# Start-up loads held in two groups, block 2's attention put one slot earlier, and the last rows' normalization moved

## The chip, the cores and the metric

The kernel runs on one core of one Trainium2 chip. The metric is the device time of one execution in microseconds (us), taken as the median of three runs. Profiled executions are separate runs; their times stand beside their spans below.

## The reference

The input x has 2 x 2048 rows of 512 numbers. Each row goes through two steps, each with a residual:

```python
x = x + layernorm(attention(layernorm(x)))
x = x + layernorm(ffn(layernorm(x)))

# attention, 16 heads of 32:
Q = h @ Wq.T + bq;  V = h @ Wv.T + bv
logits = Q . latent_keys / sqrt(32)      # 64 latent rows for each head
w = softmax(top 4 of the logits)         # the other 60 get 0
out = (w @ latent + V) @ Wo.T + bo

# ffn, 2048 experts' columns, weights rounded to -s, 0 or +s (s = mean |W|):
out = (silu(h @ Wu.T) * (h @ Wg.T)) @ Wd.T
```

All numbers are float32.

## The kernel before

The 4096 rows are taken in 8 blocks of 512 rows, each of four tiles (t = 0 to 3) of 128 rows. Weights stay in the core's memory for the whole run.

**Order of work.** Nothing is scheduled by the compiler: each engine runs its instructions in the order in which the program issues them, and every wait stops what is queued behind it on that engine. There are three parts.

1. Start-up. Block 0's attention, the rounding of the feed-forward weights and the first pieces of block 1's attention are written out by hand, step by step, in the string FIRST_STEPS. Its names are used below: `ast` (row statistics of the input), `hold` (a one-column memset on VectorE, and behind it the weight loads, which have to wait for it), `ars` (GpSimd, 1/std), `aap` (VectorE, normalizes a row tile), `atr` (four 128x128 TensorE transposes), `acp` (copies them out of PSUM), `q`/`qc` (query product and its copy), `bh`/`bl` (split the output bias; they need the load of bo), `l`/`lc` (logits and their copy), `su`/`sg`/`sd` (ScalarE: sum of |W| of one piece of a weight), `m`, `r`, `n` (VectorE: the top 4 and the softmax), `v`, `t`, `y`, `o` (values, transposes of the weights, their product, output product).
2. For each block b, the class Experts runs 16 slots (e = 0 to 15). In a slot TensorE does `up("u", e)`, `up("g", e)` and `down(e - 1)`, each 8 matmuls: the left side is split into a high and a low part, so each product is done twice. `tanh` and the cast `high` run on ScalarE; `silu`, `gate` and `low` on VectorE. Four places (0 to 3) in each slot take pieces of the next block's attention; the function `pieces` says which piece goes where. Block b's slots therefore carry block b + 1's attention and the first row statistics of block b + 2 (`after`).
3. The tail. After the last slot come the row statistics of the last block, its normalization (`z_apply`), the residual sum and the store (`z_out`).

**Turning rows into columns.** A product needs its row tile transposed. Blocks 0 and 1 do it on TensorE, for the input (tile `pt_a`) and again for the feed-forward input (`pt_f`); so does block 2 (class SecondAttention). Blocks 3 to 7 do it off TensorE: VectorE transposes 32x32 blocks (`blocks`), a DMA writes them to memory (`far_a`, `far_f`), and another loads them in column order (`a_load` into `hT`, `f_load` into `hw`).

**Shifts.** In `pieces`, `s` is 1 for blocks 3 to 7, and 0 for blocks 1 and 2: with s = 1 the attention's pieces stand one slot earlier.

**Normalization.** `Norm.apply` does it on VectorE; `Norm.shift` (one column on VectorE) with `apply_scalar` does it on ScalarE. PSUM banks come from three pools: `at_psum` (two banks), `acc_psum` (four) and the two of `up`.

**Loads.** All go through the one queue of SyncE (SP), in program order. Before, wq is loaded right behind the four row tiles; all other weights are behind `hold`.

**Last block.** In slot 1 of block 7, `y_out` normalizes and stores the four row tiles of block 6 (lines 1128 to 1130), ahead of `F.down(0)` and `F.low(1)`.

Of the kernel before, what the change touches and what calls it, by code (L numbers as in the profile page):

```python
# [17 lines left out]
P = 128  # L18
# [16 lines left out]
FIRST_STEPS = """  # L35
ast0 hold ast1 ars0_2 ast2 ars2_3 ast3 ars3_4 aap0 aap1 atr0 aap2 atr1 acp0 aap3 atr2 acp1 atr3 acp2 acp3 q0 bh
q1 qc0 bl nst0 l0 nst3 qc1 su0 nst1 v0 lc0 nst2 lc1 nrs su2 m1 su3 m0 l1 su1 r0 q2 lc2 su5 nap0
# [21 lines left out]
def latent_attention_ternary_glu(  # L59
# [15 lines left out]
    nc = tc.nc  # L75
# [84 lines left out]
    lv = wpool.tile([P, H // 2, HP], F32, name="lv")  # L160
    nc.sync.dma_start(out=wq, in_=wqT.rearrange("(c p) n -> p c n", p=P))

    def load_weights():
        nc.sync.dma_start(out=lk, in_=latk)
        nc.sync.dma_start(out=bqv_sb, in_=bqv)
        nc.sync.dma_start(out=wv, in_=wvT.rearrange("(c p) n -> p c n", p=P))
        nc.sync.dma_start(out=lv, in_=latv)
        nc.sync.dma_start(out=bo_sb, in_=bo.to_broadcast([P, D]))
        load_x(1)
        load_up("u", wuT, (0, 2, 3, 1, 5, 6, 7, 4))  # L170
        load_up("g", wgT, (1, 2, 4, 5))
# [13 lines left out]
    nc.vector.memset(ones, 1.0)  # L185
    for i in range(16):
        nc.tensor.matmul(at_psum(f"ones_{i}")[:, :P], lhsT=ones, rhs=ones, start=True, stop=True)
# [92 lines left out]
    def row(name):  # L280
        return work.tile([P, D], F32, tag="row", name=name, bufs=4)
# [9 lines left out]
    class Attention:  # L291
# [21 lines left out]
        def a_apply(self, t):  # L313
            self.norm_a.apply(normed[self.b][:, t, :], normed[self.b][:, t, :], t)
# [224 lines left out]
    class SecondAttention(Attention):  # L539
# [23 lines left out]

        def a_apply(self, t):
            self.rows["a", t] = row(f"h_a{self.b}_{t}")
            self.norm_a.apply(self.rows["a", t], normed[self.b][:, t, :], t)

        def a_trans(self, t):
            if self.hT is None:
                self.hT = transposed("X", self.b, f"hT_{self.b}", F32)  # L570
            src = transpose_row(self.rows.pop(("a", t)), f"a{self.b}_{t}")
            nc.scalar.copy(self.hT[:, :, t * P : (t + 1) * P], src)
# [3 lines left out]
    class FirstAttention(SecondAttention):  # L576
# [7 lines left out]
        def a_trans_pe(self, t):  # L584
            if self.hT is None:
                self.hT = transposed("X", self.b, f"hT_{self.b}", F32)
            self.pt = getattr(self, "pt", {})
            self.pt[t] = transpose_row(self.rows.pop(("a", t)), f"a{self.b}_{t}")

        def a_copy(self, t):  # L590
            dst, src = self.hT[:, :, t * P : (t + 1) * P], self.pt.pop(t)
            if self.b == 0 and t == 3:
                nc.vector.tensor_copy(dst, src)
            else:
                nc.scalar.copy(dst, src)
# [130 lines left out]
    class Experts:  # L726
# [85 lines left out]
        def z_apply(self, t, n=1, i=0):  # L812
            part = slice(i * D // n, (i + 1) * D // n)
            if t < TT - 1:
                nc.scalar.activation(
                    self.y[t][:, part], self.acc[t][:, part], AF.Identity,
                    bias=self.norm.nm[:, t : t + 1], scale=self.norm.rs[:, t : t + 1],
                )
            else:
                self.norm.apply(self.y[t][:, part], self.acc[t][:, part], t)  # L820

# [56 lines left out]

    def hold_weights():
        nc.vector.memset(lk[:, 0, 0:1], 0.0)  # L880
        load_weights()

# [81 lines left out]
    def pieces(A, after):  # L964
# [5 lines left out]

        if A.b > 1:
            if A.b == 2:
                put(0, 0, A.a_apply, 0)
                put(0, 0, A.a_apply, 1)
                put(0, 1, A.a_trans, 0)
                put(0, 1, A.a_trans, 1)
                put(0, 1, A.a_apply, 2)
                put(0, 1, A.a_apply, 3)
                put(0, 2, A.a_trans, 2)
                put(0, 2, A.a_trans, 3)  # L980

        s = 1 if A.b > 2 else 0
        if A.b == 2:
            put(1, 0, A.q, 0)
            put(2, 0, A.q, 1)
            put(4, 0, A.q, 2)
            put(6, 0, A.q, 3)
        elif A.b > 2:
# [27 lines left out]
        if after is not None and after.b == 2:  # L1016
            put(14, 2, after.a_stats, 0)
            put(14, 2, after.a_stats, 1)
            put(15, 1, after.a_stats, 2)
            put(15, 1, after.a_stats, 3)  # L1020
            put(15, 1, after.a_rstd, 0, 4)
        elif after is not None:
# [11 lines left out]
        put(11 - s, 2, A.o_bias, 0)  # L1034
        for t in range(1, TT):
            put(11 - s, 2, A.o, t)
            put(11 - s, 2, A.o_bias, t)
# [23 lines left out]
        else:  # L1061
            put(12, 1, A.o_rstd, 2, 4)
            put(12, 2, A.o_apply, 0)
            put(12, 2, A.o_apply, 1)
            put(13, 0, A.o_apply, 2)
            put(13, 0, A.o_apply, 3)
            put(13, 1, A.f_stats, 0)
            put(13, 1, A.f_stats, 1)
            put(13, 1, A.f_rstd, 0, 2)
            put(13, 2, A.f_stats, 2)  # L1070
            put(13, 2, A.f_stats, 3)
            put(13, 2, A.f_rstd, 2, 4)
            put(14, 0, A.f_apply, 0)
            put(14, 0, A.f_apply, 1)
            put(14, 1, A.f_alloc)
            put(14, 1, A.f_trans, 0)
            put(14, 1, A.f_trans, 1)
            put(14, 1, A.f_apply, 2)
            put(14, 1, A.f_apply, 3)
            put(15, 0, A.f_trans, 2)  # L1080
            put(15, 0, A.f_trans, 3)
        return at

    prev = None
    for b in range(NB):
# [5 lines left out]
        for e in range(EC):  # L1091
            if e == 4 and 0 < b < NB - 1:
                load_x(b + 1)
            if e == (12 if b == 0 else 6) and b + 2 < NB:
                load_normed(b + 2)
# [51 lines left out]
            if e > 0 or b < NB - 1:  # L1147
                F.low(e)
        prev = F

# [78 lines left out]
```

## Time and profile before

| what | value |
|---|---|
| median of 3 runs | 1149.09 us (1148.38 to 1149.38) |
| profiled execution | 1152.65 us, of which the span on the core is 1150.6 us |
| TensorE (PE) busy | 1134.1 us, 99% |
| VectorE (DVE) busy | 840.3 us, 73% |
| ScalarE (ACT) busy | 402.2 us, 35% |
| GpSimd (POOL) busy | 167.8 us, 15% |
| mean granted TensorE clock | 0.996 |

Times inside the profile are microseconds from the span's start. The chain of work that ended last is 93% TensorE. A group "x8" in the chain is 8 matmuls of one tile.

### The profile page before, as it was taken

What the parts mean: (1) busy time and instruction counts of PE and PEld (TensorE: products, weight loads), DVE (VectorE), ACT (ScalarE), POOL (GpSimd) and SP (SyncE); (2) the same over time, 40 slices, a digit from 0 to 9 for tenths busy, and PEclk for the clock granted to TensorE, in tenths of its full rate; (3) what the DMA queues carried; (4) which work ended last, traced back from release to release, by engine and by line L of the source; (5) the groups of instructions that cost most, each with busy time, mean ns of one, the idle gap of its engine ahead of it and who ended that gap; (6) DMA issues with size and microseconds to landing.
All of it is one profiled execution on the core that took longest, in us unless ns stands there. A gap on an engine that the chain in (4) does not pass through costs nothing.

```text
span 1150.6 us, 14497 instructions
## 1 busy us (share of the span) xinstructions
PE 1134.1 (99%) x4650; PEld 776.1 (67%) x4650; DVE 840.3 (73%) x2940; ACT 402.2 (35%) x701; POOL 167.8 (15%) x205
## 2 busy tenths in 40 slices
PE   8999999999999999999999999999999999999997
PEld 5547675776757676676657766586675776768785
DVE  5977984967966878668876788677886787847435
ACT  3995541333213322333214333143322333224223
POOL 1057001310022100320003200022002120031100
PEclk8999999999999999999999999999999999999999
DMA  9700211022211322132222232232321412102001
GB/s 350 299 0 11 65 65 46 1 95 98 65 37 37 120 83 86 43 110 92 92 74 74 74 101 92 65 97 69 115 69 55 111 67 92 62 1 74 37 1 37
DMA packets 89355, 90.87 MB, mean 79 GB/s; under 512 B 7872, under 2 KB 62400, under 8 KB 89280
## 3 DMA queue, kind: packets, MB, share of 16 engines
q1 hardware_dynamic: 89280, 89.95, 24.5%
q8 instruction: 37, 0.61, 0.2%
q14 instruction: 38, 0.31, 0.1%
HBM read 56.37 MB, written 33.55 MB: 78 GB/s over the span
## 4 chain that ended last, share of the span: by engine, by line
PE 93%; DVE 4%; DMA 1%; ACT 1%; issue 0%; SPq 0%; POOL 0%; DVEq 0%; ACTq 0%
PE pg L740 19%; PE pu L740 19%; PE acc L783 19%; PE po L468 8%; PE pv L440 8%; PE pq L353 7%; PE pv L457 3%; PE pl L367 2%; PE pq L601 2%; PE po L692 1%; PE pv L646 1%; DMA hT<-far_a 1%; DVE left L393 1%; DMA x<-in_x 0%; PE pt_f L286 0%; DVE lo L773 0%
## 5 line engine op out<-in xcount | busy, mean ns | idle before, releaser
L740 PE MATMUL pg<-hT_f,tern_g 128*128 128x512 f32 x512 | 208.1, 406 | 0.0
L740 PE MATMUL pu<-hT_f,tern_u 128*128 128x512 f32 x512 | 204.4, 400 | 0.0
L783 PE MATMUL acc<-tern_d,hi 128*128 128x512 f32 x512 | 203.6, 398 | 0.0
L783 PE MATMUL acc<-tern_d,lo 128*128 128x512 f32 x512 | 200.0, 391 | 2.2 <-DVE lo L773 2.1
L740 PE MATMUL pg<-lT_f,tern_g 128*128 128x512 f32 x512 | 199.6, 390 | 0.0
L740 PE MATMUL pu<-lT_f,tern_u 128*128 128x512 f32 x512 | 198.9, 389 | 0.0
L749 ACT ACTIVATE h<-pu,columns 128x512 f32<-128x512 f32 x128 | 87.1, 681 | 200.3 <-PE pu L740 200.1
L768 ACT CAST hi<-h 128x512 fp32r<-128x512 f32 x128 | 79.2, 619 | 216.8 <-DVE h L757 216.8
L752 DVE SCALAR_TENSOR_TENSOR h<-h,pu 128x512 f32<-128x512 f32 x128 | 85.9, 671 | 86.7 <-ACT h L749 86.7
L757 DVE TENSOR_TENSOR h<-h,pg 128x512 f32<-128x512 f32 x128 | 86.4, 675 | 66.2 <-PE pg L740 65.2
L783 PEld LDWEIGHTS acc<-tern_d,hi 128*128 128x128 f32 x512 | 96.1, 188 | 32.7 <-issue 13.4
L740 PEld LDWEIGHTS pg<-hT_f,tern_g 128*128 128x128 f32 x512 | 96.1, 188 | 25.3 <-issue 1.9
L783 PEld LDWEIGHTS acc<-tern_d,lo 128*128 128x128 f32 x512 | 96.2, 188 | 24.5 <-DVE lo L773 4.1
L740 PEld LDWEIGHTS pu<-hT_f,tern_u 128*128 128x128 f32 x512 | 96.1, 188 | 24.6 <-issue 2.6
L740 PEld LDWEIGHTS pu<-lT_f,tern_u 128*128 128x128 f32 x512 | 96.1, 188 | 22.4 <-issue 2.9
L740 PEld LDWEIGHTS pg<-lT_f,tern_g 128*128 128x128 f32 x512 | 96.2, 188 | 22.1 <-issue 3.3
L773 DVE TENSOR_TENSOR lo<-h,hi 128x512 fp32r<-128x512 f32 x128 | 92.3, 721 | 25.5 <-ACT hi L768 25.5
L440 PE MATMUL pv<-hT,wv 128*128 128x512 f32 x224 | 100.7, 592 | 0.1
L393 DVE MATCH_REPLACE8 left<-m,w 128x64 f32<-128x64 f32 x512 | 100.3, 210 | 0.0
L468 PE MATMUL po<-wo,attnT 128*128 128x512 f32 x224 | 97.3, 592 | 0.0
L353 PE MATMUL pq<-hT,wq 128*128 128x512 f32 x192 | 86.7, 594 | 1.1 <-DMA hT<-far_a 1.0
L468 PEld LDWEIGHTS po<-wo,attnT 128*128 128x128 f32 x224 | 42.5, 190 | 50.8 <-issue 48.6
(147 smaller groups left out, 1321.3 us busy)
## 6 DMA issues: line engine op xcount, KB each, us to landing
dz<-z SPq DMA_DIRECT2D x56, 256.0 KB, 2.0
wT<-dz SPq DMA_DIRECT2D x224, 64.0 KB, 1.9
x<-in_x SPq DMA_DIRECT2D x32, 256.0 KB, 3.6
out_x<-x SPq DMA_DIRECT2D x31, 256.0 KB, 2.0
xa<-in_x SPq DMA_DIRECT2D x6, 1024.0 KB, 5.2
far_a<-za SPq DMA_DIRECT2D x20, 256.0 KB, 3.0
hT<-far_a SPq DMA_DIRECT2D x20, 256.0 KB, 5.3
far_f<-zf SPq DMA_DIRECT2D x20, 256.0 KB, 2.8
```

Source lines behind the costliest of these rows:

```text
L353: nc.tensor.matmul(pq, lhsT=wq[:, k, c * P : (c + 1) * P], rhs=self.taken(k), start=(k == 0), stop=(k == DC - 1),)
L393: nc.vector.match_replace(left[:, g, :], m8[:, g, :], w[:, g, :], TAKEN)
L440: nc.tensor.matmul(self.pv[c], lhsT=wv[:, k, c * P : (c + 1) * P], rhs=self.ordered(k), start=(k == 0), stop=False,)
L457: nc.tensor.matmul(self.pv[c][pr * HP : (pr + 1) * HP, :], lhsT=lv[:, 2 * c + pr, :], rhs=self.wT.pop(2 * c + pr), start=False, stop=True, ...
L468: nc.tensor.matmul(self.po[t], lhsT=self.attnT[:, c, t * P : (t + 1) * P], rhs=wo[:, c, :], start=(c == 0), stop=(c == DC - 1),)
L740: nc.tensor.matmul(p, lhsT=tern[n, 2 * k + e // 8][:, (e % 8) * P : (e % 8 + 1) * P], rhs=self.parts[i][:, k], start=(k, i) == pairs[0], s ...
L749: nc.scalar.activation(self.h[e], self.pu[e], AF.Tanh, scale=half_u[0])
L752: nc.vector.scalar_tensor_tensor(self.h[e], self.h[e], 1.0, self.pu.pop(e), ALU.add, ALU.mult)
L757: nc.vector.tensor_tensor(self.h[e], self.h[e], self.pg.pop(e), ALU.mult)
L768: nc.scalar.copy(hi, self.h[e])
L773: nc.vector.tensor_tensor(lo, self.h.pop(e), self.hid[e][0].bitcast(F32), ALU.subtract)
L783: nc.tensor.matmul(self.acc[t], lhsT=part[:, t * P : (t + 1) * P], rhs=wd, start=(e == 0 and i == 0), stop=(e == EC - 1 and i == 1),)
```

## The change

It has these parts.

- Start-up: `hold` becomes `hold0` (behind the first tile's statistics; it holds and issues wq) and `hold1` (behind the last tile's statistics; it holds and issues all other weights). There are 20 products of ones ahead of the first transposes where there were 16. The transposes of tiles 2 and 3 go to `acc_psum` banks, and VectorE copies tile 2 where it copied tile 3.
- Block 2's attention: s is 1 for it. Its input statistics and normalization (now in place) move to slot 11 of block 0, its first two input transposes to slot 15 of block 0 and the other two to slot 0, place 1 of block 1. Its feed-forward rows are transposed by the way through memory, as in blocks 3 to 7.
- Block 1's attention (the `else` branch): the normalizations of its output and of its feed-forward input go from VectorE to ScalarE, some of it one place earlier.
- Last block: `y_out` is done two tiles in slot 1 and two in slot 2, behind `F.low`.
- Tail: the last tile is normalized on ScalarE; tile 1's residual sum moves from GpSimd to VectorE; the stores go in the order 0, 1, 2, 3.

```diff
-ast0 hold ast1 ars0_2 ast2 ars2_3 ast3 ars3_4 aap0 ...
+ast0 hold0 ast1 ars0_2 ast2 ars2_3 ast3 hold1 ars3_4 aap0 ...
...
-    nc.sync.dma_start(out=wq, in_=wqT.rearrange("(c p) n -> p c n", p=P))
-
-    def load_weights():
+    def load_weights(group):
+        if group == 0:
+            nc.sync.dma_start(out=wq, in_=wqT.rearrange("(c p) n -> p c n", p=P))
+            return
         nc.sync.dma_start(out=lk, in_=latk)
...
-    for i in range(16):
+    for i in range(20):
         nc.tensor.matmul(at_psum(f"ones_{i}")[:, :P], lhsT=ones, rhs=ones, start=True, stop=True)
...
@@ class SecondAttention
-        def a_apply(self, t):
-            self.rows["a", t] = row(f"h_a{self.b}_{t}")
-            self.norm_a.apply(self.rows["a", t], normed[self.b][:, t, :], t)
-
         def a_trans(self, t):
...
-            src = transpose_row(self.rows.pop(("a", t)), f"a{self.b}_{t}")
+            src = transpose_row(normed[self.b][:, t, :], f"a{self.b}_{t}")
...
@@ class FirstAttention
-            self.pt[t] = transpose_row(self.rows.pop(("a", t)), f"a{self.b}_{t}")
+            psum = acc_psum if self.b == 0 and t >= 2 else at_psum
+            self.pt[t] = transpose_row(self.rows.pop(("a", t)), f"a{self.b}_{t}", psum)
...
-            if self.b == 0 and t == 3:
+            if self.b == 0 and t == 2:
                 nc.vector.tensor_copy(dst, src)
...
         def z_apply(self, t, n=1, i=0):
-            if t < TT - 1:
-                nc.scalar.activation(
...
-            else:
-                self.norm.apply(self.y[t][:, part], self.acc[t][:, part], t)
+            nc.scalar.activation(
+                self.y[t][:, part], self.acc[t][:, part], AF.Identity,
+                bias=self.norm.nm[:, t : t + 1], scale=self.norm.rs[:, t : t + 1],
+            )
...
-    def hold_weights():
-        nc.vector.memset(lk[:, 0, 0:1], 0.0)
-        load_weights()
+    def hold_weights(group):
+        nc.vector.memset((lk if group else wq)[:, 0, 0:1], 0.0)
+        load_weights(group)
...
@@ def pieces(A, after)
-        if A.b > 1:
-            if A.b == 2:
-                put(0, 0, A.a_apply, 0)
...
-                put(0, 2, A.a_trans, 3)
-        s = 1 if A.b > 2 else 0
+        s = 1 if A.b > 1 else 0
         if A.b == 2:
-            put(1, 0, A.q, 0)
...
+            put(0, 1, A.a_trans, 2)
+            put(0, 1, A.a_trans, 3)
+        if s:
             put(0, 2, A.q, 0)
...
         if after is not None and after.b == 2:
-            put(14, 2, after.a_stats, 0)
...
-            put(15, 1, after.a_rstd, 0, 4)
+            for t in range(TT):
+                put(11, 2, after.a_stats, t)
+            put(11, 2, after.a_rstd, 0, TT)
...
         for t in range(1, TT):
+            if after is not None and after.b == 2:
+                put(11, 2, after.a_apply, t - 1)
+                if t == 3:
+                    put(11, 2, after.a_apply, 3)
             put(11 - s, 2, A.o, t)
             put(11 - s, 2, A.o_bias, t)
...
         else:
-            put(12, 1, A.o_rstd, 2, 4)
-            put(12, 2, A.o_apply, 0)
...
+            put(12, 0, A.o_rstd, 2, 4)
+            for t in range(TT):
+                put(12, 1 + t // 2, A.norm_o.shift, t)
+                put(12, 1 + t // 2, A.o_apply_scalar, t)
+            put(13, 0, A.f_stats, 0)
...
-            put(14, 0, A.f_apply, 0)
-            put(14, 0, A.f_apply, 1)
+            for t in range(2):
+                put(13, 2, A.norm_f.shift, t)
+                put(13, 2, A.f_apply_scalar, t)
             put(14, 1, A.f_alloc)
             put(14, 1, A.f_trans, 0)
...
+            if after is not None:
+                put(15, 2, after.a_trans, 0)
+                put(15, 2, after.a_trans, 1)
...
-            if e == (12 if b == 0 else 6) and b + 2 < NB:
+            if e == (11 if b == 0 else 6) and b + 2 < NB:
                 load_normed(b + 2)
...
-            if e == 1 and b == NB - 1:
-                for t in range(TT):
-                    prev.y_out(t)
             first("high")
...
             if e > 0 or b < NB - 1:
                 F.low(e)
+            if b == NB - 1 and e in (1, 2):
+                prev.y_out(2 * e - 2)
+                prev.y_out(2 * e - 1)
...
     F.z_rstd(3)
+    F.norm.shift(3)
+    F.z_out(1)
     F.z_apply(3, 2, 0)
     F.z_apply(3, 2, 1)
-    F.z_out(1, engine=nc.gpsimd)
+    F.z_out(2)
     F.z_out(3, 2, 0)
     F.z_out(3, 2, 1)
-    F.z_out(2)
```

More of the change, by code (lines that the diff above doesn't have):

```diff
@@ L35 @@
 FIRST_STEPS = """
-ast0 hold ast1 ars0_2 ast2 ars2_3 ast3 ars3_4 aap0 aap1 atr0 aap2 atr1 acp0 aap3 atr2 acp1 atr3 acp2 acp3 q0 bh
+ast0 hold0 ast1 ars0_2 ast2 ars2_3 ast3 hold1 ars3_4 aap0 aap1 atr0 aap2 atr1 acp0 aap3 atr2 acp1 atr3 acp2 acp3 q0 bh
 q1 qc0 bl nst0 l0 nst3 qc1 su0 nst1 v0 lc0 nst2 lc1 nrs su2 m1 su3 m0 l1 su1 r0 q2 lc2 su5 nap0
@@ L813, in z_apply @@
             part = slice(i * D // n, (i + 1) * D // n)
-            if t < TT - 1:
-                nc.scalar.activation(
-                    self.y[t][:, part], self.acc[t][:, part], AF.Identity,
-                    bias=self.norm.nm[:, t : t + 1], scale=self.norm.rs[:, t : t + 1],
-                )
-            else:
-                self.norm.apply(self.y[t][:, part], self.acc[t][:, part], t)
+            nc.scalar.activation(
+                self.y[t][:, part], self.acc[t][:, part], AF.Identity,
+                bias=self.norm.nm[:, t : t + 1], scale=self.norm.rs[:, t : t + 1],
+            )
         def z_out(self, t, n=1, i=0, engine=nc.vector):
@@ L969, in put @@
             at[e, k].append(lambda: f(*args))
-        if A.b > 1:
-            if A.b == 2:
-                put(0, 0, A.a_apply, 0)
[L974 to L979, printed above, removed]
-                put(0, 2, A.a_trans, 3)
-        s = 1 if A.b > 2 else 0
-        if A.b == 2:
-            put(1, 0, A.q, 0)
[L985 to L988, printed above, removed]
+        s = 1 if A.b > 1 else 0
+        if A.b == 2:
+            put(0, 1, A.a_trans, 2)
+            put(0, 1, A.a_trans, 3)
+        if s:
             put(0, 2, A.q, 0)
@@ L1016, in pieces @@
         if after is not None and after.b == 2:
-            put(14, 2, after.a_stats, 0)
-            put(14, 2, after.a_stats, 1)
-            put(15, 1, after.a_stats, 2)
-            put(15, 1, after.a_stats, 3)
-            put(15, 1, after.a_rstd, 0, 4)
+            for t in range(TT):
+                put(11, 2, after.a_stats, t)
+            put(11, 2, after.a_rstd, 0, TT)
         elif after is not None:
@@ L1061, in pieces @@
         else:
-            put(12, 1, A.o_rstd, 2, 4)
-            put(12, 2, A.o_apply, 0)
[L1064 to L1069, printed above, removed]
+            put(12, 0, A.o_rstd, 2, 4)
[3 more added lines that the diff above has]
+            put(13, 0, A.f_stats, 0)
+            put(13, 0, A.f_stats, 1)
+            put(13, 0, A.f_rstd, 0, 2)
             put(13, 2, A.f_stats, 2)
@@ L1077, in pieces @@
             put(14, 1, A.f_trans, 1)
-            put(14, 1, A.f_apply, 2)
-            put(14, 1, A.f_apply, 3)
+            for t in range(2, TT):
+                put(14, 1, A.norm_f.shift, t)
+                put(14, 1, A.f_apply_scalar, t)
             put(15, 0, A.f_trans, 2)
             put(15, 0, A.f_trans, 3)
+            if after is not None:
+                put(15, 2, after.a_trans, 0)
+                put(15, 2, after.a_trans, 1)
         return at
```

## The prediction

> **What bounds it now.** I read the page first, then the waits of TensorE, the chain that ended last, and the order of instructions around each wait.
>
> ```profile
> span 1150.6 us, 14497 instructions
> ...
> PE 1134.1 (99%) x4650; PEld 776.1 (67%) x4650; DVE 840.3 (73%) x2940; ACT 402.2 (35%) x701; POOL 167.8 (15%) x205
> ```
>
> TensorE is the bound: only 16.5 us of the span are not TensorE time. So three things can move the time: work taken from TensorE, one of its few waits, and the two ends where it idles. Its waits, with the longest in the last column:
>
> ```profile
> PE pt_a L286 <- DVE h_a L276: 2.4, 1, 2.4
> PE acc L783 <- DVE lo L773: 2.1, 2, 1.7
> ...
> PE pq L353 <- DMA hT<-far_a: 1.0, 1, 1.0
> PE pq L601 <- ACT ones L672: 0.8, 1, 0.8
> ```
>
> The first and last belong to the start-up, where the clock matters as well. In the windows view the granted clock is the third number from the end of a line, before the DMA share and GB/s:
>
> ```profile
> 7.40:10.80 3.40, 1.51 (x12) 1.25 (x12) 2.77 (x6) 1.06 (x2) 1.34 (x3) 1.00 1.02 349
> 10.80:14.20 3.40, 2.57 (x9) 1.56 (x7) 0.69 (x1) 0.80 (x3) 0.00 (x0) 0.50 1.05 384
> 14.20:17.60 3.40, 3.40 (x5) 1.35 (x4) 1.10 (x2) 0.62 (x1) 0.00 (x0) 0.50 1.04 399
> ```
>
> After a stretch with TensorE busy 1.51 of 3.40 us, the clock fell to 0.5 at 10.80 and came back at 17.62. The 16 query matmuls (two products) start at 12.82, go 0.85 us apart until then and 0.43 us apart later, and the first logits start at 22.24.
>
> The engines behind them are what counts, though. VectorE's top-4 work starts at 25.08, after 3.41 us of waiting, and then has no gap to speak of until 70.1; ScalarE is full from 22.93 to about 66:
>
> ```profile
> 22.93 1.05 ACT L206 ACTIVATE junk<-raw_u 128x1024 bf16<-128x1024 f32 x1
> ...
> 25.08 1.11 DVE L385 MAX8 m<-w 128x8 f32<-128x64 f32 x8 [3.41 <-ACT w L634]
> ```
>
> The last softmax step ends at 70.11 and its transposes start on TensorE at 70.38. So TensorE, VectorE and ScalarE run neck and neck from 23 to 70, and an earlier start of one alone is worth nothing.
>
> In block 1, the chain (start, duration, work):
>
> ```profile
> 349.36 0.94 PE pt_f L286 x8
> ...
> 353.97 0.88 PE pt_f L286 x8
> ...
> 357.83 6.88 DMA hT<-far_a
> 364.72 0.25 issue
> 364.96 3.24 PE pq L353 x7
> ```
>
> The sixteen `pt_f` transposes sit between matmuls, and the query product of block 3 waits for a load. Then VectorE in the last block and in the tail (start, duration):
>
> ```profile
> 1062.11 3.87 DVE L276 TENSOR_SCALAR y<-y,mv_y,rs_y 128x512 f32<-128x512 f32 x4 [0.51 <-POOL rs_y L259]
> 1065.90 1.75 DVE L773 TENSOR_TENSOR lo<-h,hi 128x512 fp32r<-128x512 f32 x1
> ...
> 1143.62 1.21 DVE L265 SCALAR_TENSOR_TENSOR nm_y<-mv_y,rs_y 128x1 f32<-128x1 f32 x1
> ```
>
> The four `y_out` stand ahead of `low`, and `low` itself is slowed from 0.69 to 1.75 us beside GpSimd's additions. In the tail a one-column operation took 1.21 us, where its two predecessors took 0.16, while GpSimd added tile 1 (1143.56 to 1144.82).
>
> **Start-up: 2.4 us gained (0.8 to 2.8).** Before, wq is issued at 2.57 and the rest from 4.33, while tiles 2 and 3 are on their way; those land at 5.67 and 7.56. By 5.6 us 1.1 MB has moved in all, which is the four tiles' 1.05 MB. With wq issued only after the first statistics (4.3), I put the last tile at about 5.7 instead of 7.56 and its statistics' end at 6.9 instead of 8.49. `hold1` then issues the rest from 6.9 instead of 4.33.
>
> The four extra products add 8 matmul records at 0.13 us, so 1.0 us: the ones end at about 7.5, as the first normalized tile arrives. At the cold rate (0.21) they would end at 8.1, off the path. The banks remove the 0.22 us wait of the third transposes for a copy. Four transposes at 0.45 us and a copy at 0.59 behind the last normalization (ends 9.0) give queries at 10.4 instead of 12.82. wq must be there: its 1 MB after the tiles at some 0.3 MB/us gives about 9.5. If it took the 7.8 us of before it would land at 12.1, which still leaves the logits at 19.
>
> At full clock the two query products take 16 x 0.43 = 6.9 us, until 17.3. The logits need `qc0`, which stands behind `bh` on ScalarE, and that waits for bo, which landed at 15.79. The queue of loads is 88% or more busy from 2 us on and never drained, so holding the loads back costs only its seams: I allow 0.45 us, so bo lands at 16.25, the first piece of raw_u at 20.25 instead of 19.80, and the logits start at 17.6. Now `su0` (first sum on ScalarE, ahead of `lc0` and `lc1`) is bounded by raw_u: 20.3 instead of 22.93. That moves VectorE's top-4 from 25.08 to about 22.65; its own work before that (bias and four statistics, 5.2 us after 16.9) ends at 22.1. TensorE is 4.6 us ahead by then, so VectorE and ScalarE set the gain: 2.4 us. Ends: 0.8 if the loads slip by 1.6 us more; 2.8 if they don't slip.
>
> **Block 2's transposes: 1.66 us gained.** The start-to-start cost of the two groups of eight `pt_f` is 0.86 + 0.80 us. The block periods confirm it: 141.8 us for block 1, 138.4 for blocks 3 to 6; 1.59 (`pt_a`) + 1.66 account for all but 0.2 us. The `pt_a` keep their cost, half of them in block 0. What replaces them is work of VectorE, SP and the DMA engines: four block transposes, four stores, eight loads. Blocks 3 to 6 carry just this with no TensorE wait over 0.1 us.
>
> **Load of hT: 1.0 us gained (0 to 1.04).** At the later boundaries the same four loads land 7.3 to 7.4 us after the first issue, and TensorE waits at most 0.03 us; here it was 8.2. Here alone no transfer runs in the 10 us before. The `hw` loads now fill that time, as in the later blocks, so I take their figure.
>
> **Last block: 1.7 us gained (1.6 to 1.85).** With `low` ahead, the 1.69 us wait at 1067.70 goes. Two `y_out` (1.9 us) then stand ahead of slot 2's `silu`, and two behind slot 2's `low`. `low` of slot 2, slowed to 1.75 us, would end near 1069; `down(2)` comes at 1071 or later. The stores leave some 5 us later, and nothing waits for them.
>
> **Tail: 0.8 us gained (0.4 to 1.1).** The one-column operation takes 0.16 instead of 1.21 us, so tile 2's `z_apply` starts at 1143.9 instead of 1144.92 and ends at 1144.65. Two half tiles on ScalarE follow (0.5 each, between its 0.29 and 0.78 rows) until 1145.6. VectorE's sums, 0.69 + 0.69 + 2 x 0.45 from 1144.2, end at about 1146.5, so the last store is issued near 1146.55 instead of 1147.30.
>
> **Costed at nothing.** In slot 11 of block 0, VectorE gets four statistics (0.87 us each) and four normalizations (0.5): 5.5 us ahead of `low`. They lie in its idle times there, 8.78 and three times 1.80 us, between the output products. They wait for the load of xa, issued at 173.37 and landed at 178.60: the statistics end at 182.1, the first output row is due at 182.77. If the load is late, VectorE's queue (output rows, then `low`) stands, and TensorE feels it through the PSUM banks after some 3 us. The normalizations on ScalarE (eight for block 1, 0.72 us each, and eight for block 2) stand ahead of `tanh` and `high`; ScalarE idles 16.43 us before `tanh` of slot 12 and is 35% busy. GpSimd's statistics move with them.
>
> **Sum.** 2.4 + 1.66 + 1.0 + 1.7 + 0.8 = 7.6 us. From the profiled execution's 1152.65 that gives 1145.05; the median of the runs is 3.56 us below that execution, so 1141.5.
>
> **Rivals.** *The clock falls again at 10.80* (0.25). The row: it fell though the stretch held 16 transposes. From 10.4, one record at 0.43, eight at 0.85 until 17.62, seven at 0.43: queries end at 20.6, 1.6 us ahead instead of 2.4. Time 1142.3. For it: the stretch's later part is transposes again. Against it: the extra products and earlier rows close the 2.38 us gap. The Trainium skill, TensorE: Matmul & The Clock Gate, Part 4: PE-mode transpose, says that transposes don't count as busy time for the clock gate; by that rule the clock falls here again. The trace can't tell: the stretch was also short of work.
>
> *The start-up gives nothing* (0.12): the held loads bring bo and raw_u 2.5 us later, as much as the hold. Then 7.6 - 2.4 = 5.2: 1143.9. Against it: the queue's 88% and more.
>
> *Slower* (0.06): block 2's new way through memory is late at the start of block 2. In the last block the corresponding split ends at 1050.37, 0.75 us before TensorE needs it at 1051.12. A delay beyond that costs in full, and above 0.75 + 7.6 = 8.35 us the change loses. Two slots late (2 x 5.44 us) gives 1141.5 + 10.1 = 1151.6. For it: one buffer serves `xa` and `hw`, and `hT` shares the queue. Against it: five blocks do it with this margin.
>
> *It does not do what it says* (0.04): wq, though held, shares the DMA with the rows as before, and new waits in blocks 0 and 1 eat the other parts: about 1149.
>
> **Numbers.** The forecast has 0.53. The ends of all terms sum to 4.4 and 8.5 us, so 1144.7 and 1140.6; with some room for a new wait of a microsecond I take 1139.8 to 1145.7, which leaves out slower and no change. A measurement of this kernel tells about 0.2%, 2.3 us, from nothing. Faster by more than that: 0.90; within: 0.04; slower: 0.06.
>
> **What would show it.** Right: the last row tile's statistics by 7 us, the first logits near 17.6, top-4 near 22.7, block 1's period near 139.2, block 2's near 138.4, no TensorE wait at slot 2 of block 7, and about 7.2 us from the last matmul's end to the span's end (8.0 before). Wrong: the first sum on ScalarE still at 22 or later, a clock of 0.5 past 14.2, or a new TensorE wait in slots 11 to 15 of block 0 or at the start of block 2.

## The result: 1145.72 us instead of 1149.09, 3.4 us less where 7.6 were forecast

| | before | after |
|---|---|---|
| median | 1149.09 us (1148.38 to 1149.64, 9 runs) | 1145.72 us (1145.06 to 1147.47, 9 runs) |
| profiled execution, and its span | 1152.65, 1150.6 us | 1146.07, 1144.2 us |
| mean granted clock in it | 0.996 | 0.999 |

The ratio is 0.9972, with a 95% interval of 0.9962 to 0.9982: faster, by less than half of what was forecast (1141.5). The median lies at the upper end of the range, just past it (1145.7). Note that the profiled executions differ by 6.58 us and the medians by 3.37. That difference turned out to be half of the story.

**The page after** (span, and busy time of each engine):

```profile
span 1144.2 us, 14526 instructions
...
PE 1131.8 (99%) x4642; PEld 775.4 (68%) x4642; DVE 830.0 (73%) x2945; ACT 414.6 (36%) x719; POOL 164.5 (14%) x204
```

TensorE's busy time fell by 2.3 us (the sixteen `pt_f` transposes of block 1 went, four products of ones came), and 12.4 us of the span are not TensorE time instead of 16.5.

**TensorE's waits after** (engine, line, what it waited for: us in total, times, longest):

```profile
PE pq L599 <- DMA wq<-in_wqT: 1.6, 1, 1.6
...
PE pt_a L287 <- DVE h_a L277: 0.7, 1, 0.7
...
PE acc L781 <- DVE lo L771: 0.4, 1, 0.4
```

The 1.69 us wait for `lo` in the last block is gone, the wait for hT at block 2 is no longer in the list, and the wait for the first normalized tile shrank from 2.4 to 0.7. A new one heads the list: the first query product waits for wq.

**The start-up after**, in the windows view (granted clock third from the end, then DMA share and GB/s):

```profile
7.40:10.80 3.40, 2.85 (x23) 2.39 (x22) 2.75 (x7) 1.59 (x4) 1.39 (x3) 1.00 0.99 303
10.80:14.20 3.40, 2.31 (x6) 1.15 (x7) 0.00 (x0) 0.27 (x2) 0.00 (x0) 1.00 1.02 339
14.20:17.60 3.40, 3.40 (x10) 1.49 (x9) 0.00 (x0) 0.00 (x0) 0.00 (x0) 1.00 1.03 299
```

The clock did not fall, and VectorE's share in the second and third stretch is 0.00: it has nothing to do there. What ScalarE and VectorE wait for is in their timelines (start, duration, work, idle time before and its releaser):

```profile
17.77 0.62 ACT L672 CAST bias<-bo_sb 128x512 fp32r<-128x512 f32 x1 [6.70 <-DMA bo_sb<-in_bo]
...
22.11 1.06 ACT L207 ACTIVATE junk<-raw_u 128x1024 bf16<-128x1024 f32 x1 [2.39 <-DMA raw_u<-in_wuT]
```

```profile
24.26 1.11 DVE L386 MAX8 m<-w 128x8 f32<-128x64 f32 x8 [0.64 <-ACT w L632]
```

ScalarE waits for bo until 17.75 and for raw_u until 22.09; both loads were forecast 1.5 to 1.8 us earlier (16.25, 20.25). So the first of my own signs of being wrong has come, a first sum on ScalarE at 22 or later. The top-4 work starts at 24.26 where I had 22.65. The chain that ended last now runs through the loads:

```profile
7.59 4.83 DMA lk<-in_latk
...
12.80 9.29 DMA raw_u<-in_wuT
22.09 0.02 issue
22.11 1.15 ACT junk L207 x2
```

Between the two loads the issue of the next rows waits for the landing of lk (at 12.41), and raw_u is issued behind those rows.

At the end of block 1, in the same view, there is no `pt_f` and no load any more, only products; the sixteen transposes and the wait have left the path:

```profile
357.60 1.81 PE pg L738 x8
359.42 1.81 PE acc L781 x8
361.23 0.12 issue
361.35 0.67 PE pq L354
```

Last, VectorE in the last block and in the tail. The `low` of slot 1 is at 0.69 us with two `y_out` behind it (slot 2 looks the same, its `low` at 1063.73), and the one-column operation of tile 2 (the third `nm_y` of the tail) takes 0.16 instead of 1.21 us:

```profile
1058.82 0.69 DVE L771 TENSOR_TENSOR lo<-h,hi 128x512 fp32r<-128x512 f32 x1 [0.69 <-ACT hi L766]
1059.43 0.99 DVE L277 TENSOR_SCALAR y<-y,mv_y,rs_y 128x512 f32<-128x512 f32 x2
...
1138.21 0.16 DVE L266 SCALAR_TENSOR_TENSOR nm_y<-mv_y,rs_y 128x1 f32<-128x1 f32 x1
```

**The account by stages.** The first up product of block 0 (`u0`) ends the start-up; the starts of the later blocks and the end of the last matmul cut the rest. "Second trace" is another profiled execution of the unchanged kernel before (experiment 1).

| stage | before, first trace | before, second trace | after |
|---|---|---|---|
| until `u0` | 89.96 | 86.79 | 89.11 |
| blocks 0 to 2 | 407.74 | 407.71 | 404.97 |
| blocks 3 to 6 | 553.43 | 553.63 | 553.57 |
| block 7 to the last matmul's end | 91.46 | 91.47 | 89.53 |
| from there to the span's end | 8.02 | 8.00 | 7.02 |

All stages but the first agree within 0.2 us between the two traces of before. After against before: 2.7 us, 1.9 us and 1.0 us gained in the three stages that the later parts touch, 5.6 in all. In the start-up the change gains 0.85 us against the first trace and **loses 2.3 us** against the second.

### The profile page after: what moved, and what is told of

The parts are those of the page before. It is cut to its first block, busy times and chain, and to the rows that moved or that the text cites. A ratio compares the mean times of both kernels' runs of the same rounds, so it can differ in the third digit from the quotient of the medians.

```text
span 1144.2 us, 14526 instructions
## 1 busy us (share of the span) xinstructions
PE 1131.8 (99%) x4642; PEld 775.4 (68%) x4642; DVE 830.0 (73%) x2945; ACT 414.6 (36%) x719; POOL 164.5 (14%) x204
## 4 chain that ended last, share of the span: by engine, by line
PE 91%; DVE 5%; DMA 2%; ACT 1%; issue 0%; SPq 0%; DVEq 0%; ACTq 0%
PE pg L738 20%; PE acc L781 20%; PE pu L738 20%; PE po L469 8%; PE pv L441 8%; PE pq L354 7%; PE pv L458 2%; PE pl L368 2%; DVE left L394 1%; PE pq L599 1%; DMA raw_u<-in_wuT 1%; PE po L690 1%; DVE m L386 1%; DVE w L396 1%; PE pv L644 1%; DMA lk<-in_latk 0%
## 5 line engine op out<-in xcount | busy, mean ns | idle before, releaser
L771 DVE TENSOR_TENSOR lo<-h,hi 128x512 fp32r<-128x512 f32 x128 | 88.8, 694 | 26.6 <-ACT hi L766 26.6
```

Of the source, the lines that this page charges most:

```text
L771: nc.vector.tensor_tensor(lo, self.h.pop(e), self.hid[e][0].bitcast(F32), ALU.subtract)
```

## The experiments

My theory after the result: (a) the parts from block 0's end onward gave what was forecast; (b) the start-up part costs some 2 us, because the held loads land later; (c) it looked like a gain because the one profiled execution of before had lost some 3 us to a fall of the clock that most executions don't have. Rivals: the later parts gave less than forecast and the start-up is neutral; or the hold is harmless and the ones or the banks cost.

**1. The kernel before, profiled again.** No edit.

> The kernel before, unchanged, profiled a second time. Theory A (the first profile of before was not a typical execution): no stretch at clock 0.5 between 10 and 18 us, a span near 1147.1 us (the median 1149.09 less the 2.05 us around the span), first up matmul of block 0 near 88 us instead of 89.96, and the load of hT at block 2 with a TensorE wait below 0.3 us. Theory B (the profile was typical and is only lifted by the recording): clock 0.5 from about 10.8 to 17.6 again, span near 1150.6, first up matmul at 90.0. Median 1149.1 by both.

Measured: 1149.51 us (11 runs) beside 1149.06 (21 runs), ratio 0.9999 (0.999 to 1.0008); the profiled one took 1149.74. The same three stretches as shown of before, in the windows view:

```profile
7.40:10.80 3.40, 2.16 (x17) 1.67 (x16) 2.34 (x6) 1.43 (x3) 1.21 (x2) 1.00 0.99 359
10.80:14.20 3.40, 2.57 (x7) 1.25 (x7) 0.69 (x1) 0.43 (x2) 0.00 (x0) 1.00 1.05 377
14.20:17.60 3.40, 3.40 (x9) 1.52 (x8) 1.12 (x2) 1.21 (x2) 0.00 (x0) 1.00 1.05 400
```

and its top-4 and first sum, in the timelines:

```profile
21.95 1.11 DVE L385 MAX8 m<-w 128x8 f32<-128x64 f32 x8 [0.30 <-ACT w L634]
```

```profile
19.80 1.06 ACT L206 ACTIVATE junk<-raw_u 128x1024 bf16<-128x1024 f32 x1 [0.23 <-DMA raw_u<-in_wuT]
```

No 0.5 in the clock column, and the top-4 starts at 21.95 instead of 25.08. raw_u landed at 19.77, as in the first trace (19.80), but here ScalarE was there and waiting. So in an execution without the fall the load already sets the start, and the 3.41 us of VectorE's waiting that I had read as the prize are not there. The two traces differ in one more thing: the last row tile landed at 7.56 us in the first and at 6.95 in the second, so TensorE waited 2.4 us for its first transposes in the first and 1.0 in the second. Of the 66 runs of before that stand beside the experiments, two have a mean clock as low as the first trace's 0.996 or lower (0.995 and 0.994: 1151.85 and 1152.32 us).

**2. Before with the start-up part alone** (two groups of loads, twenty ones, banks).

```diff
-ast0 hold ast1 ars0_2 ast2 ars2_3 ast3 ars3_4 ...
+ast0 hold0 ast1 ars0_2 ast2 ars2_3 ast3 hold1 ars3_4 ...
```

> Before with the start-up part alone (two holds, 20 products of ones, the banks, VectorE copying tile 2). Theory A: the held loads arrive about 2.3 us later (first piece of raw_u 22.09 instead of 19.80 us), and a typical execution of before had no clock loss to win back, so 0.5 to 1.5 us slower: 1149.6 to 1150.6. Theory B: 0.85 us faster as the two profiles have it (first up matmul 89.11 instead of 89.96): 1148.2. The forecast had 2.4 us faster: 1146.7.

Measured: 1150.94 us (11 runs) against 1149.06, ratio 1.0012 (1.0003 to 1.002): 1.9 us slower by the medians, 0.3 to 2.3 by the interval. raw_u landed at 20.85, the top-4 started at 23.03, `u0` at 88.22 (second trace of before: 19.77, 21.95, 86.79).

**3. The changed kernel with the start-up part undone.**

```diff
-ast0 hold0 ast1 ars0_2 ast2 ars2_3 ast3 hold1 ars3_4 ...
+ast0 hold ast1 ars0_2 ast2 ars2_3 ast3 ars3_4 ...
...
-    for i in range(20):
+    for i in range(16):
...
-            psum = acc_psum if self.b == 0 and t >= 2 else at_psum
-            self.pt[t] = transpose_row(self.rows.pop(("a", t)), f"a{self.b}_{t}", psum)
+            self.pt[t] = transpose_row(self.rows.pop(("a", t)), f"a{self.b}_{t}")
...
```

> The changed kernel with the start-up part undone (one hold, 16 products, banks and copies of before). Theory A: 0.5 to 1.5 us faster than the changed kernel, 1144.2 to 1145.2. Theory B: 0.85 us slower than it, 1146.6.

Measured: 1143.71 us (5 runs), ratio 0.9951 (0.9938 to 0.9964): 5.35 us less than the kernel before. The forecast's terms without the start-up make 1.66 + 1.0 + 1.7 + 0.8 = 5.2. So (a) holds, and by the medians the changed kernel is 2.0 us slower than itself without its first part.

**4. The changed kernel with only the hold undone**; the ones and the banks stay.

```diff
-ast0 hold0 ast1 ars0_2 ast2 ars2_3 ast3 hold1 ars3_4 ...
+ast0 hold ast1 ars0_2 ast2 ars2_3 ast3 ars3_4 ...
...
+    nc.sync.dma_start(out=wq, in_=wqT.rearrange("(c p) n -> p c n", p=P))
...
```

> The changed kernel with only the hold undone: wq issued right behind the rows, all else behind the first statistics; 20 products of ones and the banks stay. Theory A: the loads are back at their times of before (first piece of raw_u near 19.8 us) and the transposes don't wait for banks, so at least as fast as with all of the start-up part undone: 1144.0 to 1145.2. Theory B: the rows land 1.1 us later than with the hold, so slower than the changed kernel: 1146 to 1147.

Measured: 1143.94 us (5 runs), ratio 0.9949 (0.9936 to 0.9961). The whole cost is the hold's; the ones and the banks neither cost nor give anything that shows (1143.94 beside 1143.71). raw_u landed at 19.07, in a profiled execution that is the fastest of its five runs (1142.83).

**5 and 6. Which of the two holds?** In 5 both groups are issued behind the first statistics; in 6 wq is free and the rest waits for the last statistics.

```diff
-ast0 hold0 ast1 ars0_2 ast2 ars2_3 ast3 hold1 ars3_4 ...
+ast0 hold0 hold1 ast1 ars0_2 ast2 ars2_3 ast3 ars3_4 ...
```

> The changed kernel with `hold1` moved right behind `hold0`: wq and all the other loads are issued together, one behind the other, as soon as the first row tile's statistics are done; wq is still held until then. Theory A (the gap that the late second hold leaves in the load queue is what costs the 2 us): the first piece of raw_u lands at 19.1 to 19.8 instead of 22.09, the top-4 work starts 2.2 us after it (21.3 to 22.0 instead of 24.26), median 1143.8 to 1144.5. Theory B (the hold of wq itself costs, whatever stands behind it): raw_u at 21 or later, 1145.2 to 1145.9.

```diff
-ast0 hold0 ast1 ars0_2 ast2 ars2_3 ast3 hold1 ars3_4 ...
+ast0 ast1 ars0_2 ast2 ars2_3 ast3 hold ars3_4 ...
...
+    nc.sync.dma_start(out=wq, in_=wqT.rearrange("(c p) n -> p c n", p=P))
...
```

> The changed kernel with the two holds the other way about: wq is issued at once behind the rows, as before the change, and all the other loads wait for the last row tile's statistics. Theory A (the late second hold costs): raw_u lands some 2 us later than in the version with the old hold, at 21 to 22, and the median is 1145.2 to 1146.0. Theory B (the hold of wq costs): raw_u near 19.1, 1143.7 to 1144.3.

Measured: 1145.30 us (5 runs) and 1146.39 us (8 runs), beside 1149.53 for before. Neither of the two theories had it alone: experiment 5 fell between A's and B's landing times and on B's median, experiment 6 came out as A had it, 0.4 us past its range. By the medians holding wq costs 1.4 us (1145.30 - 1143.94), holding the rest 2.4 (1146.39 - 1143.94), and both together not 3.8 but 1.8. Only the second is clear of the scatter: the runs of experiment 6 (1145.64 to 1146.99) all lie above those of the two kernels with the old hold (experiments 4 and 7, 1142.83 to 1145.39), while those of experiment 5 (1144.32 to 1145.62) overlap them. That the two costs don't add up because one queue is kept short of work, once or twice, is my reading; it was not isolated. This is the one stretch from 4 to 20 us (windows view; DMA share and GB/s at the end) for experiment 4, then 5, then the changed kernel, then 6:

```profile
4.00:20.00 16.00, 15.33 (x79) 10.32 (x79) 9.58 (x23) 4.66 (x8) 2.87 (x6) 1.00 1.03 376
```

```profile
4.00:20.00 16.00, 15.30 (x79) 9.96 (x79) 8.31 (x21) 3.75 (x7) 2.83 (x6) 1.00 0.96 346
```

```profile
4.00:20.00 16.00, 14.32 (x76) 9.61 (x75) 6.98 (x18) 3.75 (x7) 2.77 (x6) 1.00 0.96 313
```

```profile
4.00:20.00 16.00, 14.97 (x76) 10.07 (x75) 7.02 (x17) 3.64 (x7) 2.87 (x6) 1.00 0.94 298
```

| kernel | GB/s from 4 to 20 us | raw_u landed | top-4 starts | `u0` | median |
|---|---|---|---|---|---|
| 4, old hold | 376 | 19.07 | 21.25 | 86.05 | 1143.94 |
| 5, both behind the first statistics | 346 | 20.39 | 22.57 | 88.32 | 1145.30 |
| the changed kernel | 313 | 22.09 | 24.26 | 89.11 | 1145.72 |
| the changed kernel again (experiment 12) | 317 | 20.97 | 23.14 | 88.55 | 1145.52 |
| 6, the rest behind the last statistics | 298 | 21.68 | 23.86 | 89.99 | 1146.39 |

In every row the top-4 starts 2.17 or 2.18 us after raw_u lands: one sum (1.06) and the two copies of the logits stand between. The landing of raw_u moves by a microsecond from one execution to the next (22.09 and 20.97 for the same kernel), so single traces rank these kernels only roughly. The medians have the same order as the bytes, but from experiment 5 to experiment 6 they lie within 1.1 us of each other.

Where the bytes are lost: in the first trace after, the changed kernel's share is 0.70 from 4 to 6 us and 0.85 from 6 to 8, against 0.96 and 1.01 in the second trace of before, some 0.8 us of the queue's time (2 x 0.26 + 2 x 0.16). That is the gap between the rows and wq. But later it moves less at a share near 1: 222 GB/s from 14 to 16 us (share 0.99) where before moved 378 (1.05). The 16 us lack 16 x (364 - 313) = 816 KB, which at the 420 GB/s of 18 to 20 us is 1.9 us, and bo and raw_u landed 2.0 and 2.3 us later than in the second trace. The second trace of the changed kernel (experiment 12) does not repeat the slow stretch: it moved 331 GB/s from 14 to 16 us (1.04), and its loss stands in the share, 0.74, 0.67 and 0.92 in the three steps from 6 to 12 us. Why the rate was low in the first was not tried. What both have is the later issue: raw_u's first piece is issued at 12.80 and 12.60 us instead of 11.60, behind lk, which waits for `hold1`. In the second trace that is nearly all of raw_u's delay (1.0 of 1.2 us), in the first about half (1.2 of 2.3).

**7. Is raw_u alone the bound?** Experiment 4 with the copies of two logits ahead of the first sum, so that the top-4 doesn't stand behind raw_u.

```diff
-q1 qc0 bl nst0 l0 nst3 qc1 su0 nst1 v0 lc0 nst2 lc1 nrs su2 ...
+q1 qc0 bl nst0 l0 nst3 qc1 nst1 v0 lc0 nst2 lc1 su0 nrs su2 ...
```

> The changed kernel with the old hold, and ScalarE's copies of the first two logits (`lc0`, `lc1`) moved ahead of its first sum (`su0`), so that VectorE's top-4 work no longer stands behind the load of raw_u. Theory (raw_u bounds the start of the top-4, 2.2 us ahead of it, and VectorE's own work before that ends at about 20.9): the top-4 starts at 20.9 to 21.0 instead of 21.25, so 0.2 to 0.4 us less than the version with the old hold alone (1143.94): about 1143.6. Rival (something else than raw_u holds the top-4, or the sums on ScalarE, begun later, become the bound): the same or up to 1 us more.

Measured: 1143.87 us (5 runs; 1143.94 without the edit): no difference. The top-4 started at 21.23, without a wait, right behind VectorE's own work, though raw_u came at 19.42. But now ScalarE runs late, in its timeline:

```profile
22.41 0.19 ACT L206 ACTIVATION_READ_ACCUMULATOR junk<-raw_u 128x1 f32 x1
23.56 1.06 ACT L206 ACTIVATE junk<-raw_u 128x1024 bf16<-128x1024 f32 x1 [0.96 <-DMA raw_u<-in_wuT]
```

and `u0` came 66.66 us behind the start of the top-4 instead of 64.80. VectorE, ScalarE and the loads are within a few tenths of each other here: taking one back moves nothing. The 1.9 us between the two stretches are not a cost of the edit, since the medians are equal: this trace is of one of the slower runs (1144.79), that of experiment 4 of its fastest.

**8. The price of the clock.** Before with 6 products of ones instead of 16.

```diff
-    for i in range(16):
+    for i in range(6):
```

> The kernel before with 6 products of ones instead of 16, so that TensorE runs dry some microseconds before the first transposes. Theory (an early fall of the granted clock, which 3 of 21 runs of the kernel before show, costs some 3 us where it happens, and a longer idle stretch before the transposes makes it happen in most runs): median 1151.5 to 1152.5, mean granted clock 0.995 or so, a stretch at 0.5 from about 10.8 to 17.6. Rival (the fall has another cause, or costs nothing while the loads bound the top-4): 1148.8 to 1149.4 and a mean clock of 0.998.

Measured: 1150.36 us (11 runs) against 1149.53, ratio 1.0012 (1.0003 to 1.0021): 0.8 us slower by the medians (0.3 to 2.4 by the interval), not 2 to 3, and not in the way I expected. Four of the 11 runs lie above 1152.5, where the 18 of before end at 1150.16. Two of the four (1152.60 and 1152.74) have a clock of 0.994 and 0.993; the other two (1152.74 and 1153.44) have 0.998, and why they are late stays open. All other runs keep 0.997 or 0.998. In its profile the clock column shows 1.00 throughout, but TensorE's timeline tells otherwise. First this kernel, then the second trace of before:

```profile
8.61 3.73 PE L286 MATMUL pt_a<-ident,h_a 128*128 128x128 f32 x16 [4.65 <-DVE h_a L276]
13.17 7.11 PE L601 MATMUL pq<-hT,wq 128*128 128x512 f32 x16 [0.83 <-ACT ones L672]
```

```profile
8.46 1.08 PE L286 MATMUL pt_a<-ident,h_a 128*128 128x128 f32 x8 [1.02 <-DVE h_a L276]
9.76 1.15 PE L286 MATMUL pt_a<-ident,h_a 128*128 128x128 f32 x8 [0.22 <-ACT hT L595]
```

After 4.65 us without work the transposes took 0.23 us apiece instead of 0.14, and the queries began at 13.17 instead of 11.74; at full rate they then took the same 7.11 us. The top-4 started at 23.05, 1.1 us later, and 3.4 us after raw_u. So a cold TensorE costs about 1 us here by the transposes alone. The first trace of before lost its 3 us with the query products at half rate as well.

**9 to 11. The other parts, each alone on the kernel before**, with the edits of the diff. First the tail:

```diff
...
-                self.norm.apply(self.y[t][:, part], self.acc[t][:, part], t)
...
+    F.norm.shift(3)
+    F.z_out(1)
...
-    F.z_out(1, engine=nc.gpsimd)
+    F.z_out(2)
```

> The kernel before with the tail of the changed kernel alone (the last normalization on ScalarE, VectorE's sums in the new order, no addition on GpSimd). Theory (the one-column operation falls from 1.21 to 0.16 us, the rest follows): 0.4 to 1.1 us less than the kernel before, 0.8 the likeliest. Rival (ScalarE's two half tiles, now behind one another, end as late as the sums did): no difference.

The `y_out` of the last block:

```diff
-            if e == 1 and b == NB - 1:
-                for t in range(TT):
-                    prev.y_out(t)
...
+            if b == NB - 1 and e in (1, 2):
+                prev.y_out(2 * e - 2)
+                prev.y_out(2 * e - 1)
```

> The kernel before with only the four `y_out` of the last block moved behind `low` of slots 1 and 2. Theory (the 1.69 us wait of the output product for `low` goes and nothing takes its place): 1.6 to 1.85 us less than the kernel before. Rival (the next output product waits instead, for `low` of slot 2 behind two of the `y_out`): 0 to 0.5 us less.

All of the edits to the attention of blocks 1 and 2 in `pieces`, with the load of xa in slot 11:

```diff
-        s = 1 if A.b > 2 else 0
+        s = 1 if A.b > 1 else 0
...
+            if after is not None and after.b == 2:
+                put(11, 2, after.a_apply, t - 1)
...
-            if e == (12 if b == 0 else 6) and b + 2 < NB:
+            if e == (11 if b == 0 else 6) and b + 2 < NB:
```

> The kernel before with only the move of block 2's first normalization to slot 11 of block 0, so that block 2 takes the way through memory as the later blocks do. Theory: the eight-fold `pt_f` transposes of block 1 go (1.66 us) and the wait for hT at the start of block 2 goes too (0.6 us in the second trace of before): 2.3 us less than the kernel before. By the forecast's terms (1.66 + 1.0) it would be 2.7. Rival (new waits in slots 11 to 15 of block 0 give part of it back): under 1.5 us less.

Measured, against 1149.24 us for before (27 runs):

| part | median | ratio, 95% interval | gain |
|---|---|---|---|
| tail | 1147.98 | 0.999 (0.9981 to 0.9999) | 1.26 us |
| `y_out` | 1147.38 | 0.998 (0.9972 to 0.9989) | 1.86 us |
| block 2 | 1146.38 | 0.9978 (0.9969 to 0.9987) | 2.86 us |

In the traces: the tail, from the last matmul's end, takes 6.87 us instead of 8.00; block 7 takes 89.48 instead of 91.47; blocks 0 to 2 take 404.85 instead of 407.71 (block 0 0.35 longer, block 1 2.72 shorter, block 2 0.49 shorter). The tail of the third kernel, which it leaves as it was, took 7.6 us in its trace, so a tail scatters by 0.4. None of the rivals with a new wait came true.

**12. The changed kernel again**, beside those three.

> The changed kernel, unchanged, beside the three parts taken alone. Theory (the start-up part costs about 2 us, the other parts give theirs): its gain is smaller than the sum of the three parts' gains by 1.5 to 2.3 us, and raw_u's first piece lands at 21 or later again. Rival (the first trace of it was an untypical one, and raw_u lands near 20 in most executions): raw_u at 19.5 to 20.5 in this profile.

Measured: 1145.52 us (6 runs), ratio 0.9969 (0.9957 to 0.998): a gain of 3.72 us where the three parts make 1.26 + 1.86 + 2.86 = 5.98. The 2.3 us between them are the start-up's cost if the gains add up; they do so only roughly, for the same parts together gave 5.35 (experiment 3), which leaves 1.6. raw_u landed at 20.97, a hair under the 21 of the theory and well above the 19.77 of before.

The traces of all runs bear it out. raw_u's first piece landed at 18.77 to 19.98 us in the nine traces of kernels with the old loads, and at 20.85 to 22.09 in the three with both holds. `u0` came at 85.75 to 87.28 in the five traces with the whole start-up of before and no fall of the clock (experiments 1, 3, 9, 10, 11), and at 88.22 to 89.11 in the three with the new one.

Two versions beat both kernels: the change without its start-up part (1143.71) and the change with the old hold (1143.94).

## Why the prediction came out as it did

**The start-up: the step that failed, twice.** I forecast a gain of 2.4 us (0.8 to 2.8, and a rival of 0); it costs about 2 (1.9 and 2.0 by the medians of experiments 2 and 3).

- *The base.* "VectorE's top-4 from 25.08 to about 22.65" was worked out against an execution in which the clock had fallen, and the result was then moved to the median by "3.56 us below that execution", as if that distance were spread over the kernel. It was the start-up alone, with the fall and the late last row tile: `u0` is 3.2 us earlier in the second trace, and every other stage is the same. So the same 3 us were taken off twice. Against the second trace's start of 21.95 (20.94 to 22.16 in the five traces named above), my own 22.65 would have been a loss of 0.7 us, and the sum 5.2 - 0.7 = 4.5, so 1144.6. The first table of the profile held the warning: the profiled execution lay 3.3 us above the slowest of the three runs.
- *The size.* "The queue of loads is 88% or more busy … so holding the loads back costs only its seams: I allow 0.45 us". raw_u landed 2.3 us later in the first trace after and 1.2 in the second. A queue that was busy before the edit does not stay so when its loads are issued later: over 4 to 20 us the share fell from 1.02 to 0.96 and 0.92 in the two traces after, and the bytes from 364 to 313 and 317 GB/s. The Trainium skill, DMA: Bandwidth & Descriptors, Rules for kernel authors, says of overlapping a load with computing to issue the DMA early and to wait on it late. Experiments 2, 4, 5 and 6 agree: holds that issue the loads 2 to 4 us later cost 1.4 to 2.4 us by the medians.
- *The rows and wq.* "I put the last tile at about 5.7 instead of 7.56", wq at "about 9.5", "queries at 10.4". Measured were 6.46, 11.75 and 11.89 (6.28, 11.49 and 11.63 in the second trace). The 7.56 was again an untypical figure: it is the latest of the ten traces in which wq is issued right behind the rows, and in the others the last tile landed at 6.01 to 7.17. So the hold brought the rows no earlier than executions differ, and wq later: 11.18 to 11.75 in the three traces with both holds, 9.39 to 10.53 in those ten. With the old hold and the twenty ones the queries started at 10.87 and 11.04 (experiments 4 and 7). The hold of wq delayed what it was meant to bring forward.
- *What held of it.* The transposes ended near 10.2, wq came near the 12.1 that I named as the late end, the first logits started at 19.03 as I had for that case, and the top-4 did start where raw_u put it.

**Block 2's transposes and hT: right in the sum, in part by luck.** Forecast 1.66 + 1.0; measured 2.86 alone, and 2.74 by the stages. Block 1 fell to 139.08 (forecast 139.2) and block 2 to 138.45 (138.4). The hT term was mis-sized against a typical execution: the wait was 1.0 us in the first trace of before and 0.6 in the second, and block 2's period fell by 0.54 there. In experiments 8, 9 and 10, which leave blocks 1 and 2 as they were, the wait is not there at all and block 2 took 138.49 to 138.56, so in such an execution this term is worth about 0.1. The statistics and normalizations in slot 11 of block 0, costed at nothing, made no TensorE wait that the list shows.

**Last block: right.** Forecast 1.7 (1.6 to 1.85); 1.86 alone, 1.94 by the stages. Two small waits of other slots went along with the large one: TensorE's waits for `lo` fell from 2.1 to 0.4 us in all.

**Tail: right.** Forecast 0.8 (0.4 to 1.1); 1.0 by the stages, 1.26 alone with an interval from 0.1 to 2.2. The span ended 7.0 us after the last matmul (forecast 7.2).

**The rivals.** *The clock falls again* did not happen: 1.00 in all three stretches, and no run of the kernels with twenty ones (49 in all) has a mean below 0.997. That is little proof of the ones' use, since before had the fall in few of its own. *The start-up gives nothing* was nearest in its mechanism, "the held loads bring bo and raw_u 2.5 us later", and its time, 1143.9, is 1.8 us short for the same reason of the base: from a typical execution such a delay is a loss and not a wash. *Slower* by the way through memory: block 2 begins with no wait for it in the first trace after and 0.2 us in the second. *Does not do what it says* (about 1149) had half of its picture right, wq not there in time (TensorE waited 1.6 us for it), but the later parts kept their gains.

## What to carry to other kernels

Before costing an edit against a profiled execution, compare that execution's time with the runs': where it lies outside them, find the stage that holds the difference, and take the terms of that stage from a second profiled execution, not from the trace as it stands. A load that is held back to let another pass is paid for by everything queued behind it; read when the last needed load is issued and when it lands, not the busy share that the queue had before the edit. Where three resources run within tenths of each other, a gain on one is bounded by the other two, but a loss on one can count in full, as it did here.

## What the runs showed of the hardware

- **The early fall of the clock is a matter of the single execution.** The first trace of before had 6.8 us at 0.5 and the second none, with the same program. The last row tile landed 0.6 us later in the first, and TensorE stood idle 2.4 us ahead of the transposes instead of 1.0; whether that made the clock fall was not isolated. The Trainium skill, TensorE: Matmul & The Clock Gate, Part 1: The HAM clock gate, says that the window in which activity is judged runs freely and does not start with the kernel; the scatter over executions agrees with that, but no run here shows the window's place.
- **The clock column can miss a cold start.** In experiment 8 it reads 1.00 while the transposes go at 0.23 us instead of 0.14; the start-to-start time of equal instructions told it. The trace records changes of the clock, and its first record there, to full speed, is at 12.58 us; the column reads 1.00 ahead of it. So it is in the other traces: in the first of before the products of ones go 0.21 us apart until the first record at 3.97, and 0.11 to 0.17 behind it.
- **Transposes seem to have warmed TensorE.** In experiment 8 the only work between 3.96 and 13.17 us was sixteen transposes at the slow rate, the record of full speed came at 12.58, and the first query products then ran at the full rate (16 in 7.11 us, as in the second trace of before). The Trainium skill, same page, Part 4: PE-mode transpose, says that transposes don't count as busy time in the same way. This one trace speaks against it, and the changed kernel, whose clock stayed at 1.00 through a stretch of transposes and idle time (8.15 to 11.89 us), does not support it either. It was not isolated.
- **A full-looking DMA queue at little more than half its rate.** 222 GB/s at a share of 0.99 from 14 to 16 us in the first trace of the changed kernel, 420 at 1.04 four microseconds later. In its second trace the same stretch moved 331 at 1.04; the cause was not tried.
